# Local correlations at 33 lags in place of two value convolutions and a contraction, in a four-block image kernel

## The chip, the cores and the metric

The kernel runs on one core of one Trainium2 chip. The metric is the device time of one execution, in microseconds (us); the median of three runs before the change is 12949.37 us (12947.43 to 12957.84). Everything is computed in float32. The engines are TensorE (PE, matrix products, written to PSUM), VectorE (DVE), ScalarE (ACT), GpSimd (POOL) and SyncE (SP, which only issues transfers). Transfers between the on-chip memory and device memory run on 16 DMA engines that all issuing engines share; in this kernel SP, ACT and POOL issue them.

## The reference

The input is a batch of 16 images of 56 x 56 positions and 128 channels. Four blocks follow each other, each with a group norm before it and a residual addition after it: a shifted-window attention, a triangle product with gates, an attention in the Fourier domain, and a "bilinear" block. The change is in the last, with a small move of weights in the second. The core of the last block:

```python
xp = silu(x @ W1) @ W2                      # 8 x 16 queries, 16 keys, 16 values
q, k, v = l2norm of each head of q, of k, of v
K_H1 = conv2d(k, H1, groups=16) + P1        # (positions, 16, 16), window 3 x 7
kernel = einsum('xnk,xkd->xnd', q, K_H1)
V    = conv2d(v, H2)                        # each value by 16 filters, 3 x 7
V_G  = conv2d(v, G) + I                     # each value by 16 filters, 3 x 7
feature = einsum('xvw,xvd->xwd', V_G, V)    # summed over the 16 values v
out  = einsum('xnd,xvd->xvn', kernel, feature)
```

At one position, with v(s) the 16 values at window place s (of 21), the feature is the sum over s and t of G[w,s] H2[d,t] times the inner product v(s).v(t), plus what I adds: I times the convolution by H2, a term linear in v. The inner product depends on a place and on the lag t - s alone; a 3 x 7 window has 33 lags up to sign.

## The kernel before

The images are taken in turn; image b uses lane b % 2. Each lane has its own working tile (the "arena", 17152 columns), 5 small tiles "w2" of 512 columns, PSUM tiles ("psb" two of one bank, "psd" one of two banks) and 12 device-memory tiles "dy". Nothing else separates the images, so two images, one in each lane, run through a stage side by side. The order of the instructions on each engine's queue, and which tile each gets, is made by a planner that simulates the run and knows the data dependencies; each queue is then executed strictly in that order, and waits are semaphores.

In the bilinear block (from L1304) an image is cut into 7 chunks of 448 positions (8 rows of 56). Per chunk:

- **project** (L1345): normalises, multiplies by W1 and W2, and takes the norms. The queries go to a "dy" tile by **kept** (L1338), which copies PSUM to a w2 tile and writes each of its 128 rows eight times side by side to device memory (1792 KB). Keys and values (32 rows, padded to 62 columns per image row, 496 per chunk) are written three times, once for each row offset of the window, to the planes "padded" (L1396).
- **spread** (L1403): four loads on SP's queue (L1406) bring the planes back with all 21 window shifts as separate partitions: 12 planes by 7 column shifts, 84 rows of 496 values each. `spread(0, q)` loads the keys, `spread(1, q)` the values, each into one half of `im`.
- **conv** (L1411): matmuls of the shifted rows with the filters. `l3wk` (keys) and `l3wg` (values by G) run as four 32-column pieces at once (**together**, L369 the first and L372 the others), `l3wf` (values by H2) as four full matmuls (L1420). ACT copies the PSUM result to a slot `zs` (L1427).
- **contract** (L1430): four loads on SP's queue (L1439) bring a "dy" tile back, one value per 8 partitions, into one of four slots `reps`; DVE multiplies each with the convolution (L1442, 128 x 1792) into one of three slots `prods`, and matmuls with a 0/1 matrix add up over the contracted index.
- **last** (L1457): the final contraction, the transposes, the scaling by the norms, the residual addition and the store (L1476).

Three contractions are made for each chunk: queries with the key convolution, that result with the `l3wf` convolution, and that with the `l3wg` convolution. Between one and the next the result goes through **kept**, that is, out to device memory and back. The rounds overlap: in round q the chunk q - 4 ends, chunk q + 2 is projected, chunk q - 2 has its second contraction and chunk q its first (L1484).

The triangle block (from L626) multiplies by four weight matrices, `w1a`, `w1b`, `gout`, `pout` (L689, L730, L731), which lie in the weight tile `wgt` that is loaded once at the start.

Of the kernel before, what the change touches and what calls it, by code (L numbers as in the profile page):

```python
# [42 lines left out]
P = 128  # L43
T = 56
# [48 lines left out]

def _constants():
# [31 lines left out]
    c["heads"] = np.kron(np.eye(8), np.ones((16, 1)))  # L126

# [78 lines left out]
def _weights(i):  # L206
# [15 lines left out]
    for n, (a, b) in zip("ab", cut):  # L222
        w["w1" + n] = np.concatenate([pw[:, a], pw[:, b], gw[:, a], gw[:, b]], 1)
    w["pout"] = g["L1_conv_p_out_w"].T
    w["gout"] = g["L1_conv_g_out_w"].T
# [48 lines left out]
    w["l3w2a"] = g["L3_conv_W2"][:128]  # L274
    w["l3w2b"] = np.pad(g["L3_conv_W2"][128:], ((0, 96), (0, 0)))
# [5 lines left out]
    wk3, wg3 = (np.zeros((P, 4, 2, 4, 8), np.float32) for _ in range(2))  # L281
    wf3 = np.zeros((P, 4, 16, 8), np.float32)
    for u in range(16):
        rows = slice(u % 4 * 21, u % 4 * 21 + 21)
        wk3[rows, u // 4, :, u % 4] = h1[u].reshape(2, 8, 21).transpose(2, 0, 1)
        wg3[rows, u // 4, :, u % 4] = gg.reshape(2, 8, 21).transpose(2, 0, 1)
        wf3[rows, u // 4, :, u % 8] = h2.reshape(16, 21).T
    wk3[84] = g["L3_conv_P1"][0].reshape(4, 4, 2, 8).transpose(0, 2, 1, 3)
    wg3[84] = g["L3_conv_I"][0].reshape(4, 4, 2, 8).transpose(0, 2, 1, 3)
    for n, v in (("l3wk", wk3), ("l3wf", wf3), ("l3wg", wg3)):  # L290
        w[n] = v.reshape(P, -1)
    return w, early, late
# [333 lines left out]
def _triangle(env):  # L626
# [38 lines left out]
    def run(b, xt):  # L665
# [3 lines left out]
        nc.gpsimd.memset(xh[:, NTOK:], 0.0)  # L669

# [12 lines left out]
        for part in range(2):  # L683
            for g in range(T // 8):
                p = e.psd()
                for i in range(8):
                    c0 = (8 * g + i) * T
                    for half, w in ((0, "w1a"), (64, "w1b")):
# [3 lines left out]
                            rhs=W(w).rearrange("p (k c) -> p k c", c=64)[:, :, HC * part : HC * part + HC],  # L692
# [34 lines left out]
        for q in range(NCH):  # L727
            s = slice(q * CH, (q + 1) * CH)
            pg, py = e.psb(), e.psb()
            mm(pg[:, :CH], lhsT=W("gout"), rhs=xh[:, s], start=True, stop=True)  # L730
            mm(py[:, :CH], lhsT=W("pout"), rhs=on[:, s], start=True, stop=True)  # L731
# [572 lines left out]
def _bilinear(env):  # L1304
# [6 lines left out]
    SPAN = 8 * PITCH  # L1311

# [3 lines left out]
    nc.gpsimd.memset(zeros[:, :part], 0.0)  # L1316
    for t in padded:
        for k in range(3):
            nc.sync.dma_start(out=t[:, k * part : (k + 1) * part], in_=zeros[:, :part])

# [4 lines left out]
    def run(b, xt):  # L1325
        nm, rs = e.group_norm(xt)
        ar = e.arena()
        kv_dram = padded[e.lane[0]]

        im = [ar[:, 4 * SPAN * k : 4 * SPAN * (k + 1)] for k in range(2)]  # L1330
        nc.gpsimd.memset(ar[64:P, 0 : 8 * SPAN], 1.0)
        zs = [ar[:, 3968 + k * 896 : 4864 + k * 896] for k in range(4)]
        reps = [ar[:, 7552 + k * 896 : 8448 + k * 896] for k in range(4)]
        prods = [ar[:, 11136 + k * 1792 : 12928 + k * 1792] for k in range(3)]
        norms = ar[:TT, 16512:16792]
# [9 lines left out]
        def project(q):  # L1345
# [17 lines left out]
            for a in range(4):  # L1363
                s = slice(a * TT, (a + 1) * TT)
                o = p[:TT, a * 32 : (a + 1) * 32]
# [118 lines left out]
        for q in range(NCH + 4):  # L1484
            if 0 <= q - 4:
                last(q - 4, *feat.pop(q - 4))
            if q + 2 < NCH:
                queries[q + 2] = project(q + 2)
            if 0 <= q - 2 < NCH:
                zf, zg = conv("l3wf", 1, 0), conv("l3wg", 1, 1 + q % 2)  # L1490
                if q - 1 < NCH:
                    spread(1, q - 1)
# [34 lines left out]
```

## Time and profile before

| what | value |
|---|---|
| median of 3 runs | 12949.37 us |
| the profiled execution's own time | 12942.02 us |
| its span (first to last instruction) | 12940.2 us |
| busy in the span: PE, DVE, ACT, POOL | 9941.9, 9365.3, 3739.1, 2346.8 us |
| mean granted TensorE clock | 0.872 |
| L1442, the contractions' multiplications on DVE | 1344 of 2019 ns, 2648.4 us |
| SP's transfers (q1) | 560000 packets, 823.91 MB, 19.1% of 16 engines |
| ACT's transfers (q10) | 365712 packets, 639.44 MB, 13.3% of 16 engines |
| POOL's transfers (q0) | 163840 packets, 616.76 MB, 17.7% of 16 engines |
| device memory read, written | 1412.69 MB, 667.03 MB |

All times come from one execution that the hardware profiler recorded. "Busy" is the union of an engine's instructions; the waits between them are put down to what ended them. A row of a group gives its source line, engine, operation, the tiles written and read, shape and count, then busy time and the mean of one. The DMA share is the mean share of time in which the 16 engines had a packet; a packet is one contiguous piece of a transfer. Queue SPq is the issuing of transfers, which is not counted as busy.

### The profile page before, as it was taken

How to read it: one execution, taken by the hardware profiler on the slowest of the kernel's cores; microseconds unless marked ns; L12 is line 12 of the kernel's file. 1: busy time of each engine (PE TensorE's matmuls, PEld its weight loads, DVE VectorE, ACT ScalarE, POOL GpSimd, SP SyncE). 2: the span in 40 equal slices, each digit the busy share in tenths (PEclk: the TensorE clock that was granted, in tenths of full speed). 3: DMA queues.
4: the chain of work that ended last, by engine and by line, in shares of the span. 5: the costliest groups of instructions: out<-in, count | busy, mean ns of one | idle time of the engine just before them, and what ended most of it. 6: DMA issues, size and time to landing. Idle time of an engine off the chain costs nothing. (4 is left out here: it accounts for less than half of the span.)

```text
span 12940.2 us, 198571 instructions
## 1 busy us (share of the span) xinstructions
PE 9941.9 (77%) x81312; PEld 5481.7 (42%) x81312; DVE 9365.3 (72%) x12257; ACT 3739.1 (29%) x6439; POOL 2346.8 (18%) x3131
## 2 busy tenths in 40 slices
PE   7787678876888767887788876878768887687876
PEld 4443254442544325443254432544325453254532
DVE  7775777757777577775877757777577775867757
ACT  4322142231422314223142231422314223142321
POOL 0133001330012300123101230012300123001230
PEclk9887888888988889888898888988889888898888
DMA  1255902659026590355903569035690356903469
GB/s 36 58 182 195 341 29 69 171 199 334 32 83 157 198 339 28 87 153 203 342 21 82 158 210 338 18 92 148 212 333 21 96 145 234 324 8 106 134 236 317
DMA packets 1090458, 2092.81 MB, mean 162 GB/s; under 512 B 97936, under 2 KB 973712, under 8 KB 1089296
## 3 DMA queue, kind: packets, MB, share of 16 engines
q1 hardware_dynamic: 560000, 823.91, 19.1%
q0 software_dynamic: 163840, 616.76, 17.7%
q10 hardware_dynamic: 365712, 639.44, 13.3%
q8 instruction: 644, 10.55, 0.3%
q14 instruction: 262, 2.15, 0.1%
HBM read 1412.69 MB, written 667.03 MB: 161 GB/s over the span
## 5 line engine op out<-in xcount | busy, mean ns | idle before, releaser
L1442 DVE TENSOR_TENSOR arena<-arena 128x1792 f32<-128x1792 f32 x1344 | 2648.4, 2019 | 652.5 <-PE psb L372 349.3
L1211 DVE TENSOR_TENSOR arena<-arena 112x1344 f32<-112x1344 f32 x1024 | 1563.3, 1552 | 322.4 <-DMA arena<-table 310.4
L372 PE MATMUL psb<-arena,cst 128*32 128x448 f32 x9792 | 1505.2, 649 | 0.0
L1209 POOL DMA_DIRECT2D arena<-table x2048 | 1050.7, 515 | 2206.3 <-DMA arena<-table 496.5
L369 PE MATMUL psb<-arena,cst 128*32 128x448 f32 x1408 | 792.3, 650 | 813.7 <-DVE arena L1442 760.4
L372 PE MATMUL psb<-arena 128*64 128x448 f32 (+2 forms) x4864 | 1248.5, 534 | 0.0
L369 PE MATMUL psb<-arena 112*64 112x448 f32 (+1 forms) x1280 | 689.0, 624 | 374.2 <-DVE arena L1104 201.9
L417 POOL TENSOR_TENSOR arena<-arena,power 112x32 f32<-112x32 f32 x224 | 828.6, 3718 | 119.8 <-DVE arena L1373 118.4
L372 PE MATMUL psd<-arena 112*64 112x224 f32 (+1 forms) x3072 | 725.6, 457 | 0.0
L372 PEld LDWEIGHTS psb<-arena 112*64 112x64 f32 (+1 forms) x4864 | 455.3, 155 | 526.8 <-issue 521.1
L1427 ACT COPY arena<-psd 128x896 f32<-128x896 f32 x336 | 304.1, 906 | 1236.1 <-DVE arena L1442 656.6
L369 PE MATMUL psd<-arena 112*64 112x448 f32 x1024 | 539.9, 612 | 133.3 <-DVE arena L1211 117.6
L369 PEld LDWEIGHTS psb<-arena,cst 128*32 128x32 f32 x1408 | 120.3, 118 | 1211.5 <-DVE arena L1442 966.4
L1104 DVE TENSOR_TENSOR arena<-w,coef 128x1792 f32<-128x1792 f32 x256 | 508.0, 2018 | 81.4 <-PE psb L372 71.0
L372 PEld LDWEIGHTS psb<-arena,cst 128*32 128x32 f32 x9792 | 360.6, 123 | 448.2 <-issue 427.4
L372 PE MATMUL psd<-arena,wgt 128*32 128x448 f32 x2688 | 502.8, 608 | 38.8 <-DMA arena<-padded 38.3
L689 PE MATMUL psd<-wgt,arena 128*64 128x128 f32 x7168 | 493.3, 283 | 49.3 <-DVE arena L701 38.9
L369 PE MATMUL psd<-arena,wgt 128*32 128x448 f32 x896 | 440.7, 611 | 79.9 <-DMA arena<-padded 42.2
L689 PEld LDWEIGHTS psd<-wgt,arena 128*64 128x64 f32 x7168 | 425.4, 139 | 179.5 <-issue 126.8
L918 PE MATMUL psb<-cst,arena 128*128 128x64 f32 (+1 forms) x2688 | 447.6, 340 | 54.3 <-ACT arena L928 25.6
L918 PEld LDWEIGHTS psb<-cst,arena 128*128 128x128 f32 x2688 | 439.0, 255 | 93.2 <-issue 50.6
L1341 ACT COPY w<-psb 128x448 f32<-128x448 f32 x336 | 178.7, 532 | 1006.5 <-PE psb L372 749.9
(305 smaller groups left out, 18845.8 us busy)
## 6 DMA issues: line engine op xcount, KB each, us to landing
arena<-table POOLq DMA_DIRECT2D x2048, 294.0 KB, 9.1
dy<-w ACTq DMA_DIRECT2D x336, 1792.0 KB
arena<-dy SPq DMA_DIRECT2D x1344, 448.0 KB
arena<-padded SPq DMA_DIRECT2D x896, 162.8 KB
w<-x SPq DMA_DIRECT2D x112, 224.0 KB
out<-w SPq DMA_DIRECT2D x112, 224.0 KB
padded<-w ACTq DMA_DIRECT2D x336, 62.0 KB
padded<-arena SPq DMA_DIRECT2D x6, 449.5 KB
```

The source lines that it names most:

```text
L369: done = mm(**first)
L372: mm(**kw)
L417: ptt(dst, src, w, ALU.pow)
L689: mm(p[half : half + 64, i // 4, i % 4 * P : (i % 4 + 1) * P], lhsT=xh[:, c0 : c0 + 64], rhs=W(w).rearrange("p (k c) -> p k c", c=64)[:, : ...
L918: mm(p[:, 2 * i * nl : 2 * (i + 1) * nl], lhsT=src[:, t * P : (t + 1) * P], rhs=fc, start=True, stop=True)
L1104: tt(t4, bc(ys[c][:, l0 : l0 + 4, :], 1, 8), bc(coef[:, c, h0 : h0 + 8, l0 : l0 + 4], 3, T), ALU.mult,)
L1209: nc.gpsimd.dma_start(out=t[hh * T : (hh + 1) * T, :], in_=bc(tflat[q, two, hh], 0, T))
L1211: tt(t4, bc(x3[:, :, s], 1, 2), t4, ALU.mult)
L1341: nc.scalar.copy(t[:, :CH], p[:, :CH])
L1427: nc.scalar.copy(z, p[:, :, :CH])
L1442: tt(t4, bc(rep, 2, 2), bc(z, 1, 2), ALU.mult)
```

## The change

The second value convolution (`l3wg`), the third contraction and the **kept** before it go. In their place:

- `project` also writes the 16 values alone, by one more small transfer, to padded planes "values". The value columns of W2 are multiplied by I at the start, so that the `l3wf` convolution gives the linear term.
- **correlate(q)** loads the values of a chunk, unshifted, eight times over 128 partitions; it squares them on ACT for lag 0. The other 32 lags are loaded from "values" at shifted addresses in 11 transfers, 16 rows for each lag, into two `reps` slots; DVE multiplies each slot with the unshifted values (128 x 992), and five matmuls with a sliding 0/1 matrix add up over the 16 values into one PSUM tile of 33 rows. ACT copies it out and writes it to the planes "corr".
- **gather(q)** brings the correlations back with the shifts that the windows need, in eight transfers of 126, 77, 28, 27, 18, 9, 18 and 9 rows into three tiles `near`.
- **feature()** adds, in one PSUM tile, the four `l3wf` matmuls and six full matmuls of `near` with `quad`, the products of the filters G and H2, which are made once at the start.
- The rounds go from 11 to 9: chunk q - 2 ends in round q.
- `quad` takes 768 columns in the constant tiles. The four triangle matrices, 768 columns as well, are no longer in `wgt`; each image loads them into its arena.

```diff
+def _lags():
+    far = ((2, -6), (1, -6), (2, 4), (1, 4), (0, 4))
+    out = [(dr, dc + k) for dr, dc in far for k in range(3)]
+    out += [(dr, dc) for dr in (2, 1) for dc in range(-3, 4)]
+    return out + [(0, 1), (0, 2), (0, 3), (0, 0)]
+
+GATHER = (
+    ((0, 15, 33, 0, 7),),
+    ((1, 22, 33, 0, 7), (2, 29, 33, 0, 7)),
+    ((0, 6, 15, 0, 3), (1, 9, 15, 0, 3), (2, 12, 15, 0, 3), (0, 0, 6, 4, 3), (1, 3, 6, 4, 3)),
+)
...
+        own, first = ar[:, 13448:14216], e.at["early"]["w1a"][1]
+        nc.sync.dma_start(out=own, in_=e.ins["early"][:, first : first + 768])
...
-            mm(pg[:, :CH], lhsT=W("gout"), rhs=xh[:, s], start=True, stop=True)
-            mm(py[:, :CH], lhsT=W("pout"), rhs=on[:, s], start=True, stop=True)
+            mm(pg[:, :CH], lhsT=own["gout"], rhs=xh[:, s], start=True, stop=True)
+            mm(py[:, :CH], lhsT=own["pout"], rhs=on[:, s], start=True, stop=True)
...
+    VPLANE, RPLANE = (T + 4) * PITCH, (T + 2) * PITCH
+    values = [e.dpool.tile([P, 16 * VPLANE // P], F32, tag=f"values{k}", name=f"values{k}") for k in range(2)]
+    corr = [e.dpool.tile([P, 928], F32, tag=f"corr{k}", name=f"corr{k}") for k in range(2)]
...
+    for n in range(3):
+        for dst, f in ((quad[:, n], 0), (scratch, 2)):
+            tt(
+                dst,
+                bc(fac[:, n, f].rearrange("p (h k) -> p h k", h=2), 2, D),
+                bc(bc(fac[:, n, f + 1], 1, 2), 3, NH),
+                ALU.mult,
+            )
+        tt(quad[:, n], quad[:, n], scratch, ALU.add)
...
+            nc.scalar.dma_start(out=planes(v_dram, (1 + 8 * q) * PITCH, ((VPLANE, D), (1, SPAN))), in_=t[32:48])
...
+        def correlate(q):
+            at = (1 + 8 * q) * PITCH
+            one, sq = e.w2()[:, :SPAN], e.w2()[:, :SPAN]
+            nc.sync.dma_start(out=one, in_=planes(v_dram, at, ((0, 8), (VPLANE, D), (1, SPAN))))
+            act(sq, one, AF.Square)
+            acc = e.psb()
+            mm(acc[:33, :SPAN], lhsT=C("slide")[:, 0:33], rhs=sq, start=True, stop=False)
+            for two in (0, 2):
+                t = reps[count[1] % 4].rearrange("p (g t) -> p g t", g=2)
+                count[1] += 1
+                for g in range(2):
+                    k, end = 8 * (two + g), 8 * (two + g) + 8
+                    row = 0
+                    while k < end:
+                        (dr, dc), n = LAGS[k], 1
+                        while k + n < end and LAGS[k + n] == (dr, dc + n):
+                            n += 1
+                        nc.sync.dma_start(
+                            out=t[row : row + D * n, g],
+                            in_=planes(v_dram, at + dr * PITCH + dc, ((1, n), (VPLANE, D), (1, SPAN))),
+                        )
+                        k, row = k + n, row + D * n
+                tt(t, t, bc(one, 1, 2), ALU.mult)
+                for g in range(2):
+                    o = 32 - 8 * (two + g)
+                    mm(acc[:33, :SPAN], lhsT=C("slide")[:, o : o + 33], rhs=t[:, g], start=False, stop=two + g == 3)
+            y = e.w2()
+            nc.scalar.copy(y[:33, :SPAN], acc[:33, :SPAN])
+            nc.scalar.dma_start(out=planes(r_dram, at, ((RPLANE, 33), (1, SPAN))), in_=y[:33, :SPAN])
+
+        def gather(q):
+            for n, parts in enumerate(GATHER):
+                row = 0
+                for s0, first, last, c0, m in parts:
+                    nc.sync.dma_start(
+                        out=near[n][row : row + (last - first) * m],
+                        in_=planes(r_dram, first * RPLANE + (8 * q + s0) * PITCH + c0, ((RPLANE, last - first), (1, m), (1, SPAN))),
                     )
+                    row += (last - first) * m
...
+        def feature():
+            p, rows, wt = e.psd(), shifted(1), W("l3wf")
+            for h in range(2):
+                for g in (2 * h, 2 * h + 1):
+                    mm(p[:, h, :CH], lhsT=wt[:, g * P : (g + 1) * P], rhs=rows[g], start=g == 2 * h, stop=False)
+            for n in range(3):
+                for h in range(2):
+                    mm(p[:, h, :CH], lhsT=quad[:, n, h], rhs=window_of(near[n]), start=False, stop=n == 2)
+            return emptied(p, 1)
...
-        queries, kern, feat = {q: project(q) for q in range(2)}, {}, {}
+        queries, kern = {q: project(q) for q in range(2)}, {}
         spread(0, 0)
-        for q in range(NCH + 4):
-            if 0 <= q - 4:
-                last(q - 4, *feat.pop(q - 4))
+        for q in range(NCH + 2):
+            if 0 <= q - 2:
+                last(q - 2, kern.pop(q - 2), feature())
             if q + 2 < NCH:
                 queries[q + 2] = project(q + 2)
-            if 0 <= q - 2 < NCH:
-                zf, zg = conv("l3wf", 1, 0), conv("l3wg", 1, 1 + q % 2)
-                if q - 1 < NCH:
-                    spread(1, q - 1)
-                feat[q - 2] = kept(contract(kern.pop(q - 2), zf)), zg
             if q < NCH:
-                zk = conv("l3wk", 0, 3)
+                correlate(q)
+            if 0 <= q - 1 < NCH:
+                gather(q - 1)
+                spread(1, q - 1)
+            if q < NCH:
+                zk = conv()
                 if q + 1 < NCH:
                     spread(0, q + 1)
                 kern[q] = kept(contract(queries.pop(q), zk))
-            if q == 0:
-                spread(1, 0)
```

## The prediction

> **What bounds the kernel now.** I read the page's busy times and its 40 slices first, then stretches of the first pair of images, then the DMA queues.
>
> ```profile
> span 12940.2 us, 198571 instructions
> ...
> PE 9941.9 (77%) x81312; PEld 5481.7 (42%) x81312; DVE 9365.3 (72%) x12257; ACT 3739.1 (29%) x6439; POOL 2346.8 (18%) x3131
> ...
> DMA  1255902659026590355903569035690356903469
> ```
>
> No engine is full over the span, so the stage that is changed has to be read alone. The DMA digits repeat every five slices, one pair of images; the 9 in each is the end of the bilinear stage of both images. By the starts of its projections (L1348) and the ends of its last additions (L1475) that stage runs from 1040.6 to 1654.8 us in the first pair; over the eight pairs it is 614 to 638 us long, 627.7 in the mean. The 190 us on both sides of it use the DMA engines at 0.02 to 0.05, so the stages hardly overlap and what the bilinear stage gains or loses comes eight times in the total.
>
> ```profile
> core 0: us, PE busy (x) PEld busy (x) DVE busy (x) ACT busy (x) POOL busy (x), PEclk, DMA share, GB/s
> 850.00:1040.00 190.00, 148.58 (x1489) 108.01 (x1492) 145.53 (x315) 89.20 (x155) 10.62 (x20) 0.79 0.05 13
> 1040.00:1100.00 60.00, 40.38 (x197) 21.78 (x191) 33.23 (x85) 24.62 (x46) 28.01 (x14) 0.74 0.43 151
> 1100.00:1350.00 250.00, 184.00 (x1068) 89.57 (x1072) 117.14 (x105) 51.29 (x91) 90.46 (x42) 0.82 0.85 295
> 1350.00:1600.00 250.00, 165.95 (x1176) 57.18 (x1168) 206.52 (x123) 34.01 (x51) 8.02 (x4) 0.86 0.96 343
> 1600.00:1655.00 55.00, 37.91 (x273) 16.65 (x270) 47.92 (x47) 12.27 (x22) 8.66 (x9) 0.82 0.74 234
> 1655.00:1850.00 195.00, 145.43 (x1716) 105.77 (x1716) 140.64 (x283) 82.79 (x166) 14.08 (x38) 0.87 0.02 6
> ```
>
> In the stage's 615 us PE is busy 428, DVE 405, while the 16 DMA engines have a share of 0.84 (60 x 0.43 + 250 x 0.85 + 250 x 0.96 + 55 x 0.74 = 519 us), and 0.96 in its long middle. The DMA engines are the bound. A busy engine moves 343 / 16 / 0.96 = 22.3 bytes per ns; I price all transfers with this.
>
> How many of the 16 engines does one transfer use? A stretch that holds four loads of 84 rows (L1406) and nothing else on SP's queue answers it:
>
> ```profile
> ## 3 DMA queue, kind: packets, MB, share of 16 engines
> q1 hardware_dynamic: 384, 0.67, 43.7%
> ```
>
> Four times 84 rows are 336 packets of 1984 bytes (0.67 MB); the other 48 are 4-byte completion records, 12 per transfer. The source of such a load is 12 planes by 7 columns by a row. 14 would divide 84 as well, and is not used: the outermost count of the source, 12, sets it. In the trace's packet records never more than 12 packets of these loads start within 74 ns, although several loads are often queued, so it is always the same 12 engines.
>
> **The change, part by part** (per chunk of 448 positions; 14 chunks per pair, 112 in all).
>
> *DVE.* Gone: the third contraction, 4 multiplications of 128x1792 at 2.02 us (L1442), 8.1 us. Added: 2 of 128x992, 2.02 x 992/1792 = 1.12 each, and one split scaling in the projection, 0.2. Net -5.6 us, 79 per pair. DVE is not the bound: worth 0 here.
>
> *PE.* Gone: 16 matmuls into 32-column strips, four at a time, and the 8 of the second value convolution. Added: 6 full matmuls of 448 columns at 0.94 us (L1420: 52.4 us for 56 in this stage) and 5 of 496, 10.8 us. The removed ones are 6.4 to 10.8 us, by whether the group's leader (L369) is counted beside its followers (L372). Net 0 to +4.4, at most 62 per pair: PE goes to 490 of some 700 us and stays hidden under the transfers; if it were not, it would cost those 62.
>
> *ACT and POOL.* A copy of 0.53 and one of 0.91 go; a square and a copy of 496 columns come, some 0.6 each; two small writes replace a large one on ACT's queue (0.4 to 0.5 us of issue each). Even. POOL's larger clearing is 1.3 us per image, under the transfers.
>
> *Transfers, total.* Gone: 1024 rows of 1792 bytes written (eight copies of the 128 rows) and 1024 read. Added, rows of 1984 bytes: values 16, unshifted load 128, lags 32 x 16 = 512, correlations 33, gather 126 + 105 + 81 = 312: 1001 rows. That is -3.67 + 1.99 MB of 13 MB.
>
> *Transfers, by engine.* The lags go in runs of equal row offset, cut into groups of 8: 3,3,2 / 1,3,3,1 / 6,2 / 5,3. A load of n lags has n as its outermost count over 16 planes. By the 12-of-84 row a run of 3 uses 3 engines with 16 rows each, one of 2 two; a single lag spreads 16 rows over 16. If these are the same first engines each time, engine 0 gets 9 x 16 + 2 = 146 rows from the lags, 16 from the unshifted load (outermost 8), 43 from the eight gathers (14+7+7+3+3+3+3+3, on 9, 11, 4, 9, 6, 3, 6 and 3 engines), 3 from the 33 correlation rows and 1 from the values: 209 rows, 415 KB. It loses 128 rows of 1792, 229 KB. Net +185 KB, +8.3 us per chunk; the last engines lose nearly 10. So the fullest engine goes from 384 x 1792 + 62 x 1984 + 56 x 512 bytes = 840 KB, 37.7 us per chunk and 527 per pair, to 46 us and 644. The other bound, an even spread, is (1.99 - 3.67) MB / 16 = -105 KB, -4.7 us per chunk. I take the uneven one: the 84-row load is the same kind of access pattern, issued by the same queue.
> The Trainium skill (DMA: Bandwidth & Descriptors, "Why a DMA increments its semaphore by 16 and not by 1") says the same more sharply: the largest number up to 16 that divides the outer counts of both sides, and always the lowest-numbered engines. It speaks against this change; no row here names an engine's number.
>
> *The stage.* Its slack over the fullest engine today: 627.7 - 527 = 101 us. By the windows the idle shares are 34 us in the first 60, 38 in the next 250, 10 in the middle, 14 at the end. First, middle and end (58) depend on chains of work and stay; the 38 can take up new transfers. The loop's 9 rounds in place of 11 shorten the end, where only 14 us idle; I count nothing for it. 644 + 58 = 702 us, +74 per pair, +595 in all. Bounds: all slack used, 644 (+130 in all); all kept, 745 (+940).
>
> *SP's queue.* SP issues 8 spread, 8 contraction loads, a load and a store now 12 + 8 + 2; then 8 + 8 + 2, 12 for the correlation and 8 gathers: 38. An 84-row load holds SP 0.76 us (median; mean 0.94), a contraction load 0.37 (mean 0.56): 28 x 0.76 + 8 x 0.37 + 1 = 25 us per chunk, at the means 32; 350 to 446 per pair, inside 702. In place of the wait for a third write (dy), the gathers wait for the correlations' write, and the spreads, contraction loads and the other image's loads are queued behind them; while the fullest engine has a backlog, that is hidden. This is the second rival below.
> The Trainium skill (same page, "Issuing engines are not separate DMA queues") calls issue time usually small relative to the transfer. The row disagrees: 0.76 us of issue against 84/12 x 1984 / 22.3 = 0.62 us of transfer. By the page SP would not matter.
>
> *Triangle weights per image.* 393 KB, 1.1 us of 16 engines, in a stage where they idle (0.02 to 0.05), before a layer norm of some 50 us; 0, and if late some 5 us for each of 8 pairs.
>
> *Setup.* Four more clearing transfers, three small loads and nine multiplications of 128x256 (0.41 us) hold one arena before the first images: 0 to 12 us once, I take 5.
>
> *Sum.* 12940 + 595 + 5 = 13540 us of span; the profiled execution's own time is 1.8 us above its span, and the median lies 7.3 above that: 13550.
>
> **Rivals.**
> - *Transfers spread evenly* (the other side). If the lags and gathers were dealt over all 16 engines, or each transfer began at another engine, the stage would shrink by 66 us per pair: 12940 - 528, some 12420; 12200 to 12750 with DVE's 79 us partly gained. It decides from the point where the fullest engine gets fewer than 115 of the 209 added rows (229 KB / 1984). For it: the bytes do fall. Against it: 12 and never more in today's 84-row loads.
> - *SP in order becomes the bound.* Its waits in the first pair's stage (without one of 280 us before it starts):
>
> ```profile
> SPq L1439 <- DVE arena L1442: 133.1, 66, 11.8
> SPq L1439 <- DMA arena<-dy: 45.3, 21, 6.8
> SPq L1406 <- DMA padded<-w: 45.1, 5, 28.8
> SPq L1406 <- DMA dy<-w: 34.2, 10, 6.4
> ```
>
> With the smaller ones they are some 390 us. With 446 of issue: 836 us per pair, +1670, 14610. Decides if the waits left exceed 702 - 446 = 256 us. Against it: the first wait is for a free buffer, which a slower stage gives.
> - *No change*: engine 0's added 117 us all fall into the slack of 101. Against it: the first 60 us cannot take them.
>
> **How the numbers follow.** Uneven engines, near 13550: 0.66, its own range 13100 to 13900. SP: 0.15, 13900 to 15000. Even spread: 0.14. Near no change: 0.05, most of it "same". The range leaves out the even spread below 12750 and half of SP's above 14500. A difference under 0.2% (26 us) can't be told from none. Faster 0.15, same 0.04, slower 0.81. The planner puts all instructions in a new order, which I can only bound by the spread of today's eight pairs, 12 us each way, 100 in all.
>
> **What would show it.** Right: a stage of about 700 us with a DMA share that falls to some 0.65 while its length grows (total bytes 11% down), mean rate near 230 GB/s, DVE idle for DMA on the correlation's multiplications; 2 to 6 completion records for each lag load. Wrong: a share of 0.9 and over 320 GB/s in a shorter stage (even spread); SP never waiting, or waiting mainly for the correlations' write, with all DMA idle meanwhile (SP); PE idle nowhere (PE the bound).

## The result: 13.4% slower, beyond the predicted range

The changed kernel takes 14694.87 us in the median (14668.49 to 14735.85, four runs); the kernel before, run beside it, 12953.6 us (12947.43 to 12963.45). The ratio is 1.1342, with a 95% interval from 1.1315 to 1.1369. The direction was forecast; 13550 us and a range up to 14500 us were not enough by far. The profiled execution took 14735.85 us, 1793.8 more than the profiled one before.

These are lines of the page of the changed kernel: span, busy times, the DMA share in 40 slices, the bytes moved, and two groups of instructions (count, busy time and mean, then the idle time ahead of them and what ended most of it).

```profile
span 14734.1 us, 195606 instructions
PE 10687.2 (73%) x78404; PEld 5828.2 (40%) x78404; DVE 8763.7 (59%) x12156; ACT 3847.7 (26%) x6534; POOL 2385.3 (16%) x3131
DMA  1346603555046550365513644236443273542735
DMA packets 983896, 1911.40 MB, mean 130 GB/s; under 512 B 105936, under 2 KB 864848, under 8 KB 982864
L1568 DVE TENSOR_TENSOR arena<-arena 128x1792 f32<-128x1792 f32 x896 | 1789.0, 2021 | 2380.5 <-DMA arena<-dy 1817.9
L1553 PE MATMUL psd<-arena,quad 128*128 128x448 f32 x1344 | 687.2, 646 | 393.8 <-DMA arena<-corr 390.3
```

Three things are to be seen. The 9 that stood in the DMA digits of every pair of images is gone: nothing reaches even 8, although the bytes fell from 2092.81 to 1911.40 MB. The contraction's multiplications (L1568, L1442 before) now stand 2380.5 us idle, 1817.9 of it until a contraction load ("arena<-dy") lands. And PE is busy 745 us longer than before, in a kernel that was meant to need fewer convolutions.

The first pair's bilinear stage, by the starts and ends that the prediction used, runs from 1107 to 1884 us. Its stretches:

```profile
core 0: us, PE busy (x) PEld busy (x) DVE busy (x) ACT busy (x) POOL busy (x), PEclk, DMA share, GB/s
1110.00:1300.00 190.00, 128.94 (x777) 63.69 (x776) 81.55 (x147) 47.59 (x89) 66.95 (x32) 0.84 0.61 201
1300.00:1600.00 300.00, 200.16 (x951) 76.84 (x951) 128.79 (x105) 41.13 (x70) 42.49 (x20) 0.81 0.71 231
1600.00:1880.00 280.00, 192.13 (x1121) 81.04 (x1120) 149.40 (x148) 46.69 (x81) 31.70 (x20) 0.82 0.58 180
```

In the middle 300 us no engine is full: PE 200, DVE 129, DMA 0.71 at 231 GB/s, where before the DMA share was 0.96 at 343. The share is the sign that the prediction gave for uneven engines: 0.64 in the mean of these stretches, against some 0.65. The mean rate is 205 GB/s and not 230, and the stage is 778 us long and not 702.

The stage also gets longer from pair to pair: 778, 896, 957, 1087, 1220, 1237, 1250 and 1197 us (614 to 638 before). The first projections of the two images of a pair start 169 us apart in the first pair and 718 us apart in the last (116 and 167 before). The images fall out of step, and one image's bilinear block then runs beside the other's attention, triangle or Fourier block. So the length of the stage no longer adds up to the total. What does: the first stage starts 66 us later than before (1107 against 1041 us), seven pair periods are 1775 us long in place of 1610 (1155 us together), and the last pair's stage, which has nothing behind it, is 572 us longer: 1793 us.

### The profile page after: what moved, and what is told of

Same layout as the page of the kernel before. It is cut to its first block, busy times and chain, and to the rows that moved or that the text cites. A ratio compares the mean times of both kernels' runs of the same rounds, so it can differ in the third digit from the quotient of the medians.

```text
span 14734.1 us, 195606 instructions
## 1 busy us (share of the span) xinstructions
PE 10687.2 (73%) x78404; PEld 5828.2 (40%) x78404; DVE 8763.7 (59%) x12156; ACT 3847.7 (26%) x6534; POOL 2385.3 (16%) x3131
## 2 busy tenths in 40 slices
DMA packets 983896, 1911.40 MB, mean 130 GB/s; under 512 B 105936, under 2 KB 864848, under 8 KB 982864
## 5 line engine op out<-in xcount | busy, mean ns | idle before, releaser
L1568 DVE TENSOR_TENSOR arena<-arena 128x1792 f32<-128x1792 f32 x896 | 1789.0, 2021 | 2380.5 <-DMA arena<-dy 1817.9
L1553 PE MATMUL psd<-arena,quad 128*128 128x448 f32 x1344 | 687.2, 646 | 393.8 <-DMA arena<-corr 390.3
L406 PE MATMUL psb<-arena,cst 128*32 128x448 f32 x6656 | 938.7, 604 | 0.0
L403 PE MATMUL psb<-arena,cst 128*32 128x448 f32 x960 | 512.9, 620 | 248.6 <-DVE arena L1568 211.4
L726 PE MATMUL psd<-arena 128*64 128x128 f32 x7168 | 517.0, 293 | 98.8 <-DVE arena L738 84.6
L1553 PEld LDWEIGHTS psd<-arena,quad 128*128 128x128 f32 x1344 | 281.1, 222 | 709.8 <-issue 356.6
L726 PEld LDWEIGHTS psd<-arena 128*64 128x64 f32 x7168 | 447.3, 148 | 210.2 <-issue 136.3
L634 PE MATMUL psb<-cst,arena 128*49 128x128 f32 x2048 | 359.8, 330 | 231.3 <-DVE arena L629 142.6
L1421 PE MATMUL psb<-w,wgt 128*128 128x448 f32 x448 | 285.5, 738 | 271.6 <-DVE w L1416 267.6
L581 POOL TENSOR_SCALAR arena<-xt,sm 128x21 f32<-128x21 f32 (+4 forms) x288 | 164.8, 584 | 1844.2 <-PE psb L599 1619.4
L1507 PE MATMUL psb<-arena,cst 128*33 128x496 f32 x896 | 431.9, 626 | 6.3 <-DVE arena L1504 6.3
```

Source lines behind the costliest of these rows:

```text
L403: done = mm(**first)
L406: mm(**kw)
L634: nc.tensor.transpose(p[:WIN, i * P : (i + 1) * P], s3[:, 4 * g + i, :], C("ident"))
L726: mm(p[half : half + 64, i // 4, i % 4 * P : (i % 4 + 1) * P], lhsT=xh[:, c0 : c0 + 64], rhs=own[w].rearrange("p (k c) -> p k c", c=64)[:, ...
L1507: mm(acc[:33, :SPAN], lhsT=C("slide")[:, o : o + 33], rhs=t[:, g], start=False, stop=two + g == 3)
L1553: mm(p[:, h, :CH], lhsT=quad[:, n, h], rhs=window_of(near[n]), start=False, stop=n == 2)
```

## The experiments

Three theories stood at the start. **A**: the lag loads use few of the 16 DMA engines (as the prediction supposed, always the same ones; the trace names no engine). **B**: a chain of work from round to round inside an image (lag loads, product, sum, write, gather, feature) is too long for the two rounds that it has. Part of it even lies in one round: by the kernel's text the last row that gather(q - 1) reads is one that correlate(q) writes in the same round. **C**: SP, which issues 38 transfers per chunk, is the bound. After the second set two more were added: **D**, TensorE's added work is not hidden, and **F**, the correlation holds two of the four `reps` slots, in which the contraction loads land. Experiments that share a set were run beside the same runs of the kernel before; ratios are to that kernel, so a difference of 0.01 between ratios is about 130 us.

### Set 1: few engines, the round's order, the weights

**e1: one lag per transfer.** 32 loads of 16 rows in place of 11 of 16 to 96 rows; the same bytes, three times the transfers, but an outermost count of 16.

```diff
                         (dr, dc), n = LAGS[k], 1
-                        while k + n < end and LAGS[k + n] == (dr, dc + n):
-                            n += 1
                         nc.sync.dma_start(
```

> The changed kernel with each lag loaded by a transfer of its own: 32 loads of 16 rows per chunk, each on 16 engines, in place of 11 loads of 16 to 96 rows on 2 to 6 engines. Rows, bytes and everything behind them stay. Theory A (the fullest DMA engine sets the time, as I predicted): engine 0 falls from 209 added rows to 32 + 16 + 43 + 4 = 95, below the 115 at which the even-spread case begins, so 12400 to 13000 us. Theory B (a chain of work from round to round inside one image sets it: lag loads, product, sum, write, gather, feature, last contraction, and then the slots for the next lag loads): 14500 to 14900, since no link gets shorter. Theory C (SP's issue time sets it): 21 more loads at 0.42 us, 9 us per chunk and 112 chunks, 15200 to 15700.

Measured: 14011.96 us, 1.0809 [1.0764, 1.0854], 683 us less than the changed kernel. The same multiplications in the page of e1:

```profile
L1566 DVE TENSOR_TENSOR arena<-arena 128x1792 f32<-128x1792 f32 x896 | 1784.7, 2020 | 1433.0 <-DMA arena<-dy 833.1
```

Their idle time for contraction loads falls from 1817.9 to 833.1 us, though no contraction load was touched: those loads share the engines, and the slots, with the lag loads. Which of the two passes the delay on, this run does not separate. A holds for 5.3 of the 13.4 per cent, but not as it was stated: if the fullest engine alone had set the time, e1 would have come out at 13000 us or less. SP's issuing takes some 460 us of each stage here, some 370 in the changed kernel, and the time falls all the same, which speaks against C.

**e2: gathers and the value spread one round later**, ahead of the correlation of that round; the last contraction is a round later too.

```diff
-        for q in range(NCH + 2):
-            if 0 <= q - 2:
-                last(q - 2, kern.pop(q - 2), feature())
+        for q in range(NCH + 3):
+            if 0 <= q - 3:
+                last(q - 3, kern.pop(q - 3), feature())
             if q + 2 < NCH:
                 queries[q + 2] = project(q + 2)
+            if 0 <= q - 2 < NCH:
+                gather(q - 2)
+                spread(1, q - 2)
             if q < NCH:
                 correlate(q)
-            if 0 <= q - 1 < NCH:
-                gather(q - 1)
-                spread(1, q - 1)
```

> The changed kernel with the gathers and the value spread of a chunk one round later, ahead of the correlation in their round, so that the correlations they read were written a round before; the last contraction is one round later too (chunk q - 3 in round q, 10 rounds). All loads, sizes and engines as they were. Theory A (fullest DMA engine): 14500 to 14900, no row moves to another engine. Theory B (chain from round to round): the write, its landing, the gather's issue and landing and the feature's matmuls, together some 20 to 30 us per chunk, leave the chain; with 56 chunks one after the other in a lane 1100 to 1700 us, so 13000 to 13600. Theory C (SP's issue time): within 100 us of the changed kernel's 14700.

Measured: 14441.85 us, 1.1141 [1.1091, 1.119], 253 us less. B holds for 2.0 per cent, far less than the 1100 to 1700 us that it had been given. The quadratic matmuls, which sat 390.3 us idle for the gathers in the changed kernel, hardly wait any more:

```profile
L1553 PE MATMUL psd<-arena,quad 128*128 128x448 f32 x1344 | 549.3, 551 | 32.2 <-DMA arena<-corr 31.8
```

**e3: both edits.**

> Both edits: one lag per transfer, and the gathers one round later. Theory A: as the first edit alone, 12400 to 13000. Theory B: as the second edit alone, 13000 to 13600, plus up to 200 for the longer issue. Theory C: 15200 or more. If A and B each hold a part, less than either edit alone.

Measured: 13919.53 us, 1.0738 [1.0693, 1.0782]. The two gains overlap: 775 us in place of 936, so behind e1 the later round is worth 92 us only. The stages stay at 779 to 843 us over the eight pairs: the drift of the images goes with these two edits, and some 960 us of loss are left without it.

**e4: the kernel before with the triangle weights loaded per image**, and nothing else of the change.

> The kernel before with one part of the change alone: the four triangle matrices are loaded by each image into its arena, not once at the start. My prediction had this at nothing (under cover of the layer norm), at most 5 us for each of 8 pairs: 12950 to 12990 us, ratio 1.000 to 1.003. If the per-image load were part of the loss, each of 16 images would wait for it, 10 us or more: 13110 or more.

Measured: 12947.44 us, 0.9984 [0.9959, 1.0009]. This part of the change costs nothing that can be measured.

### Set 2: SP's issuing, and all lag loads

**e5: five lag loads of 128 rows.** Each brings 16 planes by 8 column shifts, the planes outermost; a 0/1 matrix picks the wanted lags in the sum. SP issues 27 loads fewer per chunk than in e1. The price is 640 rows in place of 512, and multiplications of 2480 columns in place of 1984.

```diff
+GROUPS = ((2, -6), (2, -1), (1, -6), (1, -1), (0, 0))
...
+                    dr, dc = GROUPS[two + g]
+                    nc.sync.dma_start(out=t[:, g], in_=planes(v_dram, at + dr * PITCH + dc, ((VPLANE, D), (1, 8), (1, SPAN))))
...
+                    mm(acc[:33, :SPAN], lhsT=C("pick")[:, o : o + 33], rhs=t[:, g], start=two + g == 0, stop=two + g == 4)
```

> The changed kernel with the lags loaded in five transfers of 128 rows (16 planes outermost, 8 neighbouring lags inside, lag 0 and seven lags that are used twice or not at all among them), each on 16 engines, in place of 11 transfers; the square on ACT goes, a fixed 0/1 matrix per group picks the 33 lags. 640 rows in place of 512, multiplications of 2480 columns in place of 1984. One lag per transfer gave 14012 with 32 loads of about 0.45 us on SP. Theory A+C (uneven engines, and after that SP's issue time): 27 fewer loads, some 12 us per chunk and 112 chunks if SP is the bound all the time, 1350 us; at the 0.6 to 0.75 of the stage in which SP was issuing, 800 to 1000: 13000 to 13200. Theory A alone (engines): 13900 to 14100, as with one lag per transfer. Theory B (chain inside an image): 13800 to 14000, a few us less issue in the chain.

Measured: 13948.25 us, 1.0753 [1.0666, 1.084]. The interval holds e1's ratio: 27 issues less per chunk bring nothing that these runs can tell. A small gain could hide behind the added rows and columns; e7 has no such price.

**e6: e5 with e2's later gathers.**

> The five transfers of 128 rows, and the gathers and value spreads one round later as in the second run of the first set. There the delay gave 253 us on the changed kernel and 92 us on one lag per transfer. Theory A+C: 50 to 150 below the grouped kernel without delay, 12900 to 13100. Theory B: 250 us or more below it.

Measured: 13705.61 us, 1.0566 [1.0493, 1.0639]. The later gathers bring 243 us here, with even lag loads, against 92 in e3; with two runs each, these two can't be told apart with any certainty. What is left over the kernel before is 738 us.

**e7: e6 with the gathers issued by POOL.**

```diff
-                    nc.sync.dma_start(
+                    nc.gpsimd.dma_start(
                         out=near[n][row : row + (last - first) * m],
```

> The grouped loads and the delay, with the eight gathers issued by POOL in place of SP; POOL is idle for most of the stage. Theory C (SP's issue time still counts): 8 x 0.8 us per chunk leave SP, 6.4 us, up to 700 us in all, at SP's share in the stage 300 to 450 less than with the gathers on SP. Theory A or B: within 100 us of it, or slower where POOL's own 7 us steps wait behind a gather that waits.

Measured: 13734.47 us, 1.0588 [1.0517, 1.066], the same as e6 within the intervals, where C had 300 to 450 us less. C falls.

**e8: the changed kernel with lag loads only in the first chunk of each image.**

> The changed kernel without its lag loads except in the first chunk of each image: later chunks multiply what lies in the slots, so the features are not computed. Multiplications, sums, writes, gathers and feature stay. This bounds what the lag loads cost in engines, issue and waiting together. If they are the whole loss (theories A and C): 12700 to 13000. If the added matmuls, the gathers and the chain carry a part (theory B, or PE): 13300 or more.

Measured: 13860.36 us, 1.0685 [1.0613, 1.0757]. Without the lag loads of six of the seven chunks 834 of some 1740 us go. So the lag loads could not be the whole story; half of the loss is there without them.

### Set 3: TensorE and the slots

e6 is the base of three of these, since A and B are mended in it.

**e9: the kernel before with six more full matmuls per chunk**, overwritten by the ones that it makes anyway.

```diff
+                    for g in range(3):
+                        mm(p[:, h, :CH], lhsT=wt[:, g * P : (g + 1) * P], rhs=rows[:, g], start=True, stop=True)
```

> The kernel before with six more full 128 x 448 matmuls per chunk (the number that the quadratic part adds), their results overwritten, nothing else changed. Open is the rest of the loss, some 740 us in e6 (13705.6), after the engine counts and the round's order are mended. Theory D, the added TensorE work is on the path (the prediction had put it at nothing, at most 62 us per pair of images): 672 matmuls of about 0.8 to 1.1 us, so +400 to +700 us here, 13350 to 13650. Theory E, the rest lies in the way of the values through memory (gathers, lag loads, rep slots): the matmuls are hidden by DVE's and the DMAs' work, 12940 to 13050.

Measured: 13450.02 us, 1.0383 [1.0341, 1.0425], 499 us. The contraction's multiplications in the page of the kernel before, and then of e9:

```profile
L1442 DVE TENSOR_TENSOR arena<-arena 128x1792 f32<-128x1792 f32 x1344 | 2648.4, 2019 | 652.5 <-PE psb L372 349.3
```

```profile
L1444 DVE TENSOR_TENSOR arena<-arena 128x1792 f32<-128x1792 f32 x1344 | 2663.9, 2020 | 942.7 <-PE psb L372 490.9
L1420 PE MATMUL psd<-arena,wgt 128*128 128x448 f32 x1344 | 566.1, 555 | 13.1 <-ACT arena L1429 8.7
```

The idle time of the multiplications grows by 290 us: by 142 where they wait for the contraction's matmuls, by 70 where they wait for loads, by 60 where they wait for ACT's copy of the convolution. Of PE's added 574 us busy (10515.7 against 9941.9) 499 appear in the total: they were not hidden under the transfers, although the DMA engines are what is fullest in that stage. The price is shown; the way it takes is spread over several waits.

**e10: e6 without the six quadratic matmuls and with one of the five that sum the lags.**

```diff
-                for g in range(n):
-                    o = 33 * (two + g)
-                    mm(acc[:33, :SPAN], lhsT=C("pick")[:, o : o + 33], rhs=t[:, g], start=two + g == 0, stop=two + g == 4)
+            mm(acc[:33, :SPAN], lhsT=C("pick")[:, 132:165], rhs=t[:, 0], start=True, stop=True)
...
-                    mm(p[:, h, :CH], lhsT=wt[:, g * P : (g + 1) * P], rhs=rows[g], start=g == 2 * h, stop=False)
-            for n in range(3):
-                for h in range(2):
-                    mm(p[:, h, :CH], lhsT=quad[:, n, h], rhs=window_of(near[n]), start=False, stop=n == 2)
+                    mm(p[:, h, :CH], lhsT=wt[:, g * P : (g + 1) * P], rhs=rows[g], start=g == 2 * h, stop=g == 2 * h + 1)
```

> e6 without the six quadratic matmuls per chunk and with one of the five matmuls that sum the lags; all transfers and multiplications stay (the output lacks the quadratic features). TensorE busy about 1060 us less. D: most of e6's 740 us go, 12950 to 13200. E: at most 200 us go, 13500 to 13700.

Measured: 13259.23 us, 1.0234 [1.0193, 1.0276]: 446 us less than e6, between the two expectations. D holds, but is not alone. The edit also removes matmuls that hold `reps` slots, so D and F were still mixed.

**e11: e6 with gathers only for the first chunk of each image.**

```diff
-            for n, parts in enumerate(GATHER):
+            for n, parts in enumerate(GATHER if q == 0 else ()):
```

> e6 with the gathers of the correlations only for the first chunk of each image; every matmul and lag load stays (the later chunks' features are computed from the first chunk's correlations). D: within 100 us of e6, 13600 to 13720. E with the gathers as its part: 13250 to 13500.

Measured: 13684.72 us, 1.0559 [1.0521, 1.0598], the same as e6. The eight gathers of a chunk, in uneven shares on 3 to 11 engines, cost nothing that these runs can tell once they are made a round later.

**e12: e6 with the lag products in the product slots.** The loads' slots are then free when DVE has multiplied, and not when PE has summed.

```diff
-                tt(t, t, bc(one, 1, n), ALU.mult)
+                made = prods[count[2] % 3][:, : n * SPAN].rearrange("p (g t) -> p g t", g=n)
+                count[2] += 1
+                tt(made, t, bc(one, 1, n), ALU.mult)
...
-                    mm(acc[:33, :SPAN], lhsT=C("pick")[:, o : o + 33], rhs=t[:, g], start=two + g == 0, stop=two + g == 4)
+                    mm(acc[:33, :SPAN], lhsT=C("pick")[:, o : o + 33], rhs=made[:, g], start=two + g == 0, stop=two + g == 4)
```

> e6 with the lag products written to the product slots in place of over the loaded values, so that a rep slot comes free with VectorE's multiplication and not with the matmul behind it. Theory F, the rep slots that the correlation holds (SP waits 534 us for its matmuls and 380 us for its multiplication at the rep loads in e6) set the pace: -150 to -350 us, 13350 to 13550. If not: 13650 to 13780.

Measured: 13386.54 us, 1.0321 [1.0282, 1.0359], 319 us less than e6. F holds. In e6's waits of SP's queue (time, count, longest), the contraction loads (L1558) wait for the matmuls that sum the lags (L1500):

```profile
SPq L1558 <- PE psb L1500: 533.9, 183, 12.7
SPq L1558 <- DVE arena L1497: 380.1, 74, 12.2
```

In e12 the first of these is gone, and the second, the wait for the lag products (L1499 there), grows:

```profile
SPq L1560 <- DVE arena L1499: 543.5, 206, 8.8
```

The contraction's multiplications, idle for late loads in e6, are idle for PE in e12, as they were in the kernel before. First e6, then e12:

```profile
L1561 DVE TENSOR_TENSOR arena<-arena 128x1792 f32<-128x1792 f32 x896 | 1787.1, 2021 | 1480.5 <-DMA arena<-dy 1048.0
```

```profile
L1563 DVE TENSOR_TENSOR arena<-arena 128x1792 f32<-128x1792 f32 x896 | 1779.0, 2020 | 872.7 <-PE psb L409 575.0
```

### Set 4: does it add up?

**e13: e12 with e10's matmuls taken away**, all transfers and multiplications kept.

> e12 (13386.5) without the six quadratic matmuls per chunk and with one of the five matmuls that sum the lags (the output lacks the quadratic features); transfers and multiplications stay. If TensorE's work and the rep slots add up to all of e6's loss: 12900 to 13050, the kernel before within 1%. If e10's gain was partly that of the slots (it removed matmuls that held them) and something else is left: 13150 to 13300.

Measured: 13029.77 us, 1.0068 [1.0042, 1.0094], inside the first expectation. With even loads, later gathers, free slots and without the added matmuls, all but 0.7 of the 13.4 per cent is gone. Its pair period is 1606 us, that of the kernel before 1610; its span is 80 us longer, by a later start and a longer last stage. It is no finished kernel: it has less work on PE than even the kernel before (9814 against 9942 us).

```profile
span 13020.4 us, 189674 instructions
...
PE 9814.2 (75%) x76164; PEld 5439.0 (42%) x76164; DVE 8833.0 (68%) x12268; ACT 3777.1 (29%) x6426; POOL 2445.2 (19%) x3131
```

**e14: the changed kernel with e12's product slots alone**, its loads on few engines as they are.

```diff
-                tt(t, t, bc(one, 1, 2), ALU.mult)
+                made = prods[count[2] % 3][:, : 2 * SPAN].rearrange("p (g t) -> p g t", g=2)
+                count[2] += 1
+                tt(made, t, bc(one, 1, 2), ALU.mult)
```

> The changed kernel with the lag products written to the product slots, so that a rep slot comes free with VectorE's multiplication; the loads stay as they are, on few engines. F adds up with the rest: 14350 to 14500 (-200 to -350). If the loads' uneven engines hide it (a slot is late by its load, not by its release): 14600 to 14750. More product slots taken in turn could also cost: up to 14850.

Measured: 14297.31 us, 1.1049 [1.102, 1.1077], 2.9 per cent less than the changed kernel; more than expected. Among SP's waits at the contraction loads of the changed kernel were these two:

```profile
SPq L1565 <- DVE arena L1568: 445.0, 214, 8.7
SPq L1565 <- PE psb L1507: 385.2, 88, 22.7
```

The second, the wait for the matmuls of the lag sums, is absent from e14.

**e15: the changed kernel without the six quadratic matmuls.**

```diff
-                    mm(p[:, h, :CH], lhsT=wt[:, g * P : (g + 1) * P], rhs=rows[g], start=g == 2 * h, stop=False)
-            for n in range(3):
-                for h in range(2):
-                    mm(p[:, h, :CH], lhsT=quad[:, n, h], rhs=window_of(near[n]), start=False, stop=n == 2)
+                    mm(p[:, h, :CH], lhsT=wt[:, g * P : (g + 1) * P], rhs=rows[g], start=g == 2 * h, stop=g == 2 * h + 1)
```

> The changed kernel without the six quadratic matmuls per chunk (the output lacks the quadratic features), all else kept, the gathers too. TensorE busy about 690 us less. D adds up: about -400 to -550, 14150 to 14300. If in the changed kernel the late transfers hide TensorE's work, as the prediction had it: 14550 to 14700.

Measured: 14290.88 us, 1.1047 [1.1002, 1.1091], 2.95 per cent or some 380 us less than the changed kernel by the ratios (404 by the medians), even where the loads are late. PE's busy time falls by 259 us only (10428.0), and not by the 687 of the matmuls' own row: other matmuls of the stage are recorded longer, above all the contractions' (first the changed kernel, then e15):

```profile
L406 PE MATMUL psb<-arena,cst 128*32 128x448 f32 x6656 | 938.7, 604 | 0.0
```

```profile
L406 PE MATMUL psb<-arena,cst 128*32 128x448 f32 x6656 | 1040.3, 657 | 0.0
```

The price was read from the total for that reason, not from busy time.

**The account.** Four single edits on the changed kernel, in per cent of the time before:

| cause | run | its part of 13.42 |
|---|---|---|
| lag loads on few engines | e1 | 5.33 |
| six quadratic matmuls per chunk on PE | e15 | 2.95 |
| `reps` slots held until the lag sums are made | e14 | 2.93 |
| gathers and value spread a round too soon | e2 | 2.01 |
| sum | | 13.22 |

Each part is uncertain by about 0.5, and e3 shows that parts can overlap (5.33 and 2.01 gave 6.04 together), so the close sum is partly luck. Every edit also gives the planner a new order of all instructions; e4, e7 and e11, whose edits showed no effect, lie within 0.3 per cent of their bases. That is all that is known of what a new order costs by itself; the parts of the table are larger. Made together, in e13, the mendings leave 0.68, and e13 also goes without four of the five lag sums. The table has costs only. What the change saves (a contraction, a convolution, 8.7 per cent of the bytes) and what else it adds are not separated; together they come out near zero in e13. The best version with the whole computation, e12, is still 3.2 per cent slower than the kernel before, and most of what is left there is PE's work: e13 takes it away and 2.5 of the 3.2 go.

## Why the prediction failed

**Right: the number of DMA engines per transfer.** By the prediction's rule a chunk's transfers on SP's queue leave 377 completion records in the changed kernel (96 of the spreads, 128 of the contraction loads, 62 of the lag loads, 8 of the unshifted load, 51 of the gathers, 16 each of the load and the store). With 112 chunks and 16 weight loads that is 42480; the packet records of the trace have 43168 of 4 bytes on that queue, and the 688 left over are those of 49 transfers of the setup. In e1 a chunk's lag loads should leave 512 in place of 62, which is 50400 more; the trace of e1 has 93568, exactly that. The Trainium skill's rule (DMA: Bandwidth & Descriptors, "Why a DMA increments its semaphore by 16 and not by 1"), that the outermost counts set the number of engines, agrees with this count. A rule of the same page ("Rules for kernel authors") asks for an outermost count that is a multiple of 16; e1 does just that, and gains 5.3 per cent.

That it is always the same engines is not shown. The prediction read it from never more than 12 packets of the 84-row loads starting within 74 ns, but the same records have up to 13 in 75 ns and 16 in 80 ns, and no record names an engine.

**Right in kind, not in size: the uneven engines.** The +595 us lie near the 683 that e1 gains, but the two are not the same quantity, and their closeness is luck. The +595 are against the kernel before, with its rows taken away; e1 is against the changed kernel. By the prediction's own count e1 takes engine 0 from 209 added rows to 95. At 1984 bytes a row and 22.3 bytes per ns those 114 rows are 10.1 us per chunk, some 1140 us in all; e1 got 683. So the fullest engine sets the time for a part only.

**Right: the triangle weights** at 0 (e4), **the bytes** (1911.40 against 2092.81 MB, or -188 MB without the new weight loads' 6 MB, as reckoned), **SP's issuing** (some 370 us per pair, forecast 350 to 446) and the DMA share of the stage. The lag products were to be seen waiting for loads, and are (174 us for the unshifted and the lag loads); the larger wait showed at the contraction's multiplications, which share the slots and the engines.

**Wrong: "PE goes to 490 of some 700 us and stays hidden under the transfers".** This is the first failed step. The prediction gave the price of PE's net added work, at most 62 us per pair if not hidden, 496 us in all, and put 0 into the sum. e9 measured 499 us for the six matmuls in the kernel before, e15 some 380 in the changed one. That 496 and 499 agree is chance, since the 496 also have the lag sums added and the removed matmuls taken off; PE's busy time in fact rose by 745 us. The reason given, that another resource is fuller, does not make a cover. The page before already showed that the multiplications' largest idle time, 349.3 of 652.5 us, was for PE; the prediction did not show that row, and looked at shares.

With this goes its premise, "The DMA engines are the bound". e9 moves the same data and is 3.8 per cent slower. In e13 the fullest engine gets, by the prediction's count, 95 of the added rows (40 of the lags, 8 unshifted, 43 of the gathers, 4 written), fewer than the 115 below which the kernel was to get faster. It moves 153 MB less than the kernel before and is 0.7 per cent slower. So the saved bytes bought nothing that can be seen.

**Wrong: the slots, which the prediction never priced.** It listed the lag loads as bytes and engine time. But these loads take two of the four slots in turn with the contraction loads, and because the product is written over the loaded values, a slot is held until a matmul has read it. Before, a slot was free after one multiplication. That is 2.9 per cent (e14), 319 us with even loads (e12), and no term of the sum has it.

**Wrong: "First, middle and end (58) depend on chains of work and stay".** The new chain (lag loads, product, sum, copy, write, gather, feature) has to end within two rounds. In the changed kernel it did not: the quadratic matmuls stand 390.3 us idle for the gathers, 31.8 in e2. The prediction counted nothing for the loop of 9 rounds and let the new order cost 100 us at most either way. A round more brings 253 us (e2); with even loads it brings 92 (e3) or 243 (e6). Together with PE's work and the slots that is 7.9 per cent, some 1020 of the 1145 us by which the forecast fell short, as far as the parts add up.

**Wrong: "the stages hardly overlap and what the bilinear stage gains or loses comes eight times in the total".** It was true of the kernel before, and was taken as a law. In the changed kernel the stages are 3600 us longer together (8622 against 5022) and the total only 1741, since one image's block runs beside another's earlier blocks. e11 shows it plainly: its stages are 898 us long in the mean, those of e6 805, and the two take the same time. The pair period alone does not add up either: it is 1643 us in e11 and 1685 in e6, and e11's last stage is 253 us longer. First start, seven periods and last stage have to be taken together.

**The rivals.** The even spread did not come, for the reason that the prediction gave; what it would have brought was too high as well, as e13 shows. "SP in order" has a time, 14610 us, that lies near the result by luck, since half of its mechanism is false: issuing costs nothing that can be seen (e5, e7). The half on waits was nearer: SP's queue does wait for free buffers, and some of those waits are F. The rival set them aside with "the first wait is for a free buffer, which a slower stage gives". A slower stage does not free a buffer sooner if what makes it slow holds the buffer. On issue time the skill's section "Issuing engines are not separate DMA queues" calls it usually small, where the prediction's row of 0.76 us, against an estimate of 0.62 us for the transfer, said otherwise. The row stands, but e5 and e7 show that the page's conclusion is the one that holds here: fewer or moved issues change nothing that can be told.

**The setup** was put at 0 to 12 us. The first attention matmul starts 16 us later (80 against 64 us). The rest of the 66 us by which the first stage starts late lies somewhere in the blocks ahead of it; its cause stays open.

## What to carry to other kernels

PE, 70% busy inside a chain of dependent steps, was not covered here by fuller DMA engines: before work is put on it, look for rows in which others wait for it, and price the addition at its full time as one end of the range. Where new transfers land in buffers that old ones use, price the buffers as well as the bytes: what frees each, and when; here a product written to another tile was worth 2.9 per cent. And put a dimension of 16 outermost in a transfer where there is one: with the lags outermost, in runs of up to 6 over 16 planes, the loads cost 5.3 per cent more here than one by one.

## What the runs showed of the hardware

TensorE's granted clock mostly went with how busy it was. In the order of its busy share: 0.830 in the changed kernel (72.5%), 0.828 in e15 (73.0%), 0.844 in e14 (74.1%), 0.854 in e1 (75.5%), 0.872 in the kernel before (76.8%), 0.862 in e6 (77.7%), 0.876 in e12 (78.9%). e10 with 0.833 at 75.0% and e13 with 0.844 at 75.4% lie below their neighbours. Which of the two leads, these runs do not show, since a lower clock also changes the busy time. Nor does the busy time of the same matmuls simply follow the clock. These are the same 78404 records in the changed kernel (0.830), in e2 (0.842) and in e12 (0.876):

```profile
PE 10687.2 (73%) x78404; PEld 5828.2 (40%) x78404; DVE 8763.7 (59%) x12156; ACT 3847.7 (26%) x6534; POOL 2385.3 (16%) x3131
```

```profile
PE 10807.0 (75%) x78404; PEld 5848.9 (41%) x78404; DVE 8782.4 (61%) x12156; ACT 3812.3 (26%) x6511; POOL 2328.7 (16%) x3131
```

```profile
PE 10507.4 (79%) x78404; PEld 5738.7 (43%) x78404; DVE 8843.4 (66%) x12268; ACT 3744.0 (28%) x6398; POOL 2412.6 (18%) x3131
```

How much of the total is due to the lower clock, these runs don't separate. The Trainium skill (TensorE: Matmul & The Clock Gate, "Part 1: The HAM clock gate") says that an idle array is throttled and that activity lifts it, which has the same direction.
